# All stores of two steps ahead of the keys, and positions between gelus: one edit to a convolution and window-attention kernel

## The chip, the cores and the metric

The kernel runs on one core of a Trainium2 chip. The time is device microseconds of one execution; lower is better. The core has a tensor engine (TensorE, PE in the profile), VectorE (DVE), ScalarE (ACT), GpSimd (POOL) and SyncE (SP), which here only issues DMA transfers. Each engine works through its own list of instructions in order, and semaphores tie the lists together.

## What is computed

The input x has shape (4, 16, 512, 512), float32. Four layers follow each other; the edit is in the first one, layer 0:

```python
pos = depthwise_conv3x3(x, pos_w)                 # one filter a channel
x = x + pos + pos_b
y = (x @ color1.T) * alpha1 + beta1               # tokens of 16 channels
q, k, v = split(windows_8x8(y) @ qkv_w.T + qkv_b) # 2 heads of 8 channels
out = softmax(q * 8**-0.5 @ k.T) @ v              # inside each 8 x 8 window
x = x + out @ proj_w.T + proj_b
h = gelu(((x @ color2.T) * alpha2 + beta2) @ fc1_w.T + fc1_b)   # 64 hidden
x = x + h @ fc2_w.T + fc2_b
```

Layer 1 quantizes x and its weights to 8 bits, convolves 3 x 3, normalizes over the batch and clips to 0 to 6. Layer 2 is two 3 x 3 convolutions with a relu between them and a residual sum. Layer 3 is a 3 x 3 convolution, a perceptron with 128 hidden channels and a residual sum. The kernel returns the float32 result of layer 3.

## The kernel before

Layer 0 is the function `window_attention`. It runs 64 steps, n = 0 to 63. A step covers, for each of the 4 images (index u) and each of 8 strips of the picture, 8 rows by 64 columns, which is 8 windows. The strips lie on the partitions: four groups of 32 (index vv), each with two strips of 16 channels.

All lists of instructions are in the order of the source (a manual schedule, no planner). A step is put together from these parts, by their names in the code:

- `depthwise(n, tap, u)` (L287): four small matmuls that add one of nine taps for image u into PSUM bank u. Banks 0 and 1 are one tile (`pairs[0]`), banks 2 and 3 another (`pairs[1]`).
- `position(n)`: when all 36 groups of a step are issued, VectorE copies banks 0 and 1 (L302) and ScalarE banks 2 and 3 (L298) with the bias into a tile `y`.
- `turn_keys(y, vv)` (L310): eight DMA transfers of 32 KB that bring one fourth of `y` into the tile `y2`, by which keys and values are read. They are the "keys". They go through SP.
- `query` (L319): the queries, multiplied with the key weights, into the tile `g`.
- `values(k)` (L338): four transposes of `y2` into bank 4 or 6, copied on into a tile `yt`. `scores(k, n)` (L353): the scores of one eighth of the step into banks 0 to 3, and their exponentials on ScalarE (L361). `attend` (L374) multiplies exponentials and values; `divide` (L389 to L396) and `turn_back` (L403) bring the result into the tile `o`.
- `project(y)` (L409, L414): the output projection and the residual sum into `y`.
- `hidden(y, u, vv, b, n)` (L421): a perceptron block, four matmuls into one of banks 4 to 7 and a gelu on ScalarE (L426). A step has 16.
- `output(...)` (L432, L437): the second half of the perceptron for 16 blocks, and four sums by VectorE into the tile `xo`. It is issued in the next step, behind `scores(0)`.

The work of several steps is interleaved: step n attends its own windows, turns the keys of step n + 1, and forms the depthwise sums of step n + 2. `xo` holds two steps side by side: the even one writes the left half of its columns, the odd one the right half; there is a single buffer (L554). `output` of an odd step is issued in the even step behind it, and there `store` puts 32 stores of 64 KB on a list. `send(k)` takes up to k stores from the list and issues them on SP (L90). `highest_output` (L452) takes the absolute maximum of one eighth of `xo` on VectorE.

The middle of a step is a loop over k = 1 to 7. At its end, in this order: the keys of step n + 1 (at k = 1, 3, 5 and 7), one `highest_output`, and `send(5)` (L537 to L539). An even step so issues 8 keys and 10 stores in turn, and 2 stores at the end; an odd step has no stores. Behind all this SP issues the load of x for step n + 4 (1320 KB, L185).

The end of a step is written as a string (L561). Its letter at place i stands for a depthwise group (d), a perceptron block (h) or a query (q), and i % 4 gives the group of 32 rows of the array that it uses, the image of a d and the vv of an h. Perceptron blocks take banks 6, 7, 4 and 5 in turn. With the last d `position(n + 2)` is issued at once. The last thing of a step on ScalarE is the table load for the exponentials (L574); the load for gelus is at L540.

Of the kernel before, what the change touches and what calls it, by code (L numbers as in the profile page):

```python
# [86 lines left out]
def _store_block(nc, x1, src, b, r0, cols, queues=None):  # L87

    rows = x1.rearrange("m (r c) b x -> (m r) c b x", r=2)[r0 + 1 : r0 + 1 + WS, :, b, cols]
    (next(queues) if queues else nc.sync).dma_start(rows.rearrange("m c x -> c m x"), src)  # L90
# [53 lines left out]
def window_attention(ctx: ExitStack, tc, xw, x1, hots, m, v, peak):  # L144
# [15 lines left out]
    U = V = 4  # L160
# [122 lines left out]
    def depthwise(n, tap, u):  # L283

        dy, dx = divmod(tap, 3)
        for vv in range(V):
            nc.tensor.matmul(  # L287
                bank(u)[quad(vv)], taps[quad(u), tap, :],
                xts[n][quad(u), vv, dy : dy + WS, dx : dx + BW],
                start=tap == 0, stop=tap == 8,  # L290
            )

    def position(n):

        y = px.tile([P, U, N], F32, tag="y", name=f"y{n}", bufs=3)
        for u in range(U):
            if u // 2:
                nc.scalar.activation(  # L298
                    by_window(y[:, u]), by_row(bank(u)), AF.Identity, bias=v("pos_b")
                )  # L300
            else:
                nc.vector.tensor_scalar(  # L302
                    by_window(y[:, u]), by_row(bank(u)), v("pos_b"), None, ALU.add
                )
        return y

    def turn_keys(y, vv):
        for u in range(U):
            for w in range(2):
                nc.sync.dma_start(  # L310
                    y2[32 * u + C * w : 32 * u + C * w + C, vv, :, w, :],
                    y[32 * vv + C * w : 32 * vv + C * w + C, u, :].rearrange(
                        "p (j t) -> p j t", t=T
                    ),
                )

    def query(y, h, vv, b, scalar=False):
        for u in range(U):
            nc.tensor.matmul(  # L319
                b[quad(u)], wg[h][quad(vv)], y[quad(vv), u, :], start=True, stop=True  # L320
            )
        out, src = g[:, vv, :, h, :], b.rearrange("p (j t) -> p j t", t=T)
        if scalar:
            nc.scalar.activation(out, src, AF.Identity, bias=gb[:, h : h + 1])
        else:
            nc.vector.tensor_scalar(out, src, gb[:, h : h + 1], None, ALU.add)
# [6 lines left out]
    def values(k):  # L333

        vv, jl = k // 2, 4 * (k % 2)
        b, t = bank(4 + 2 * (k % 2)), yts[k % 3]
        for jj in range(4):
            nc.tensor.transpose(  # L338
                b[:, P * jj : P * jj + P],
                y2[:, vv, jl + jj].rearrange("p w t -> p (w t)"), m("ident"),  # L340
            )
        src = b.rearrange("p (a w c) -> p a w c", w=2, c=C)
        if 0 < k < 7:
            nc.scalar.copy(t[:, :, 0:3:2], src)
        else:
            nc.vector.tensor_copy(t[:, :, 0:3:2], src)  # L346

    def scores(k, n):

        vv, jl = k // 2, 4 * (k % 2)  # L350
        for i, jj in ((0, 0), (0, 1), (1, 0), (0, 2), (1, 1), (0, 3), (1, 2), (1, 3)):
            for u in (2 * i, 2 * i + 1):
                nc.tensor.matmul(  # L353
                    bank(u)[:, P * jj : P * jj + P],
                    y2[quad(u), vv, jl + jj].rearrange("p w t -> p (w t)"),
                    g[quad(u), vv, jl + jj].rearrange("p h t -> p (h t)"),
                    start=True, stop=True,
                )
        e = px.tile([P, U, 4, P], F32, tag="e", name=f"e{n}_{k}", bufs=3)
        for i in range(2):  # L360
            nc.scalar.activation(  # L361
                e[:, 2 * i : 2 * i + 2].rearrange("p u j t -> p u (j t)"),
                pairs[i], AF.Exp,
            )
        return e

    def attend(e, k):

        t = yts[k % 3]
        for jj in range(4):  # L370
            for u in range(U):
                for w in range(2):
                    half = slice(64 * w, 64 * w + 64)
                    nc.tensor.matmul(  # L374
                        bank(4 + 2 * (k % 2) + w)[quad(u), P * jj : P * jj + P],
                        t[half, U * jj + u, w : w + 2].rearrange("p d c -> p (d c)"),
                        e[half, u, jj, :],
                        start=True, stop=True,
                    )

    def part(t, k):
        vv, jl = k // 2, 4 * (k % 2)
        return t[:, vv, jl : jl + 4].rearrange("p j h t -> p (j h t)")
# [18 lines left out]
    def turn_back(t, k):  # L402
        nc.vector.transpose(part(o, k), t.rearrange("p b w c -> p (b w c)"))  # L403
# [25 lines left out]
    def output(y, xo, hids, us, banks, n):  # L429

        for k, (vv, hd) in enumerate(hids):
            nc.tensor.matmul(  # L432
                bank(banks[k // 4])[quad(vv)], m("fc2"), hd, start=True, stop=True
            )
        at = BW * (n % 2)
        for u, i in zip(us, banks):
            nc.vector.tensor_tensor(  # L437
                xo[:, u, :, at : at + BW].rearrange("p a (j x) -> p a j x", x=WS),
                by_window(bank(i)), by_window(y[:, u]), ALU.add,
            )  # L440
        if n % 2:
            store(xo, n // 2, us)
# [22 lines left out]
    def send(k, queues=None):  # L465
        for _ in range(min(k, len(stores))):
            src, u, r, cb = stores.pop(0)
            _store_block(nc, x1, src, u, r, slice(XW * cb, XW * cb + XW), queues)
# [40 lines left out]
    for n in range(STEPS):  # L509
        more, ahead = n + 1 < STEPS, n + 2 < STEPS  # L510
        taken, asked = [0] * U, [0] * V

        def block(what, i, b, scalar=False):
            at = i % 4
            if what == "q" and more:
                query(ys[n + 1], asked[at], at, b, scalar)
                asked[at] += 1
            elif what == "d" and ahead:
                depthwise(n + 2, taken[at], at)
                taken[at] += 1  # L520
                if taken == [9] * U:
                    ys[n + 2] = position(n + 2)

        values(0)
        es, ts = {0: scores(0, n)}, {}
        if last:

            output(*last)
        for k in range(1, 8):
            es[k] = scores(k, n)  # L530
            values(k)
            attend(es[k - 1], k - 1)
            ts[k - 1] = divide(k - 1, n, nc.gpsimd)
            if 1 < k < 7:
                turn_back(ts[k - 2], k - 2)
            if k % 2 and more:
                turn_keys(ys[n + 1], k // 2)  # L537
            highest_output()
            send(5)  # L539
        nc.scalar.preload_act_table_set("gelu_and_others")  # L540
        attend(es[7], 7)
        ts[7] = divide(7, n, nc.gpsimd)
        for k in (5, 6, 7):
            turn_back(ts[k], k)
        free = iter((4, 5, 6, 7, 4, 5))
        for i, what in enumerate("qqddddqqqqdddddd"):
            block(what, i, bank(next(free)) if what == "q" else None, True)
        if more:
            highest(n + 1)
        highest_output()  # L550
        y = ys.pop(n)
        project(y)
        if n % 2 == 0:
            xo = px.tile([P, U, WS, XW], F32, tag="xo", name=f"xo{n}", bufs=1)  # L554
        if not more:
            flag = bounded()

        hids, units = [], itertools.cycle((6, 7, 4, 5))  # L560
        for i, what in enumerate("ddddhdhddhqhddhqhddhdhddhdhddhdhddhdhddddhdh"):  # L561
            if what == "h":
                q = len(hids)
                hids.append(hidden(y, q // 4, i % 4, bank(next(units)), n))
                if not more and q in (5, 9, 13):
                    u = q // 4 - 1
                    output(y, xo, hids[q - 5 : q - 1], (u,), (u,), n)
                    send(8, queues)
            else:
                block(what, i, bank(next(units)) if what == "q" else None)  # L570
        if n + 4 < STEPS:
            xts[n + 4] = load(n + 4)
        if more:
            nc.scalar.preload_act_table_set("natural_log_exp_and_others")  # L574
        last = (y, xo, hids, range(U), (5, 4, 6, 7), n)
# [797 lines left out]
```

## Time and profile before

| | us |
|---|---|
| median of 3 runs | 5752.89 |
| lowest and highest of them | 5740.05, 5767.73 |
| the profiled execution | 5755.15 |
| its span, first to last instruction | 5753.4 |
| TensorE busy | 5477.8 |
| VectorE busy | 3734.7 |
| ScalarE busy | 3491.1 |
| layer 0, to the end of the last sum of L437 | 3262.6 |
| granted TensorE clock, mean | 0.987 |

How to read it: the busy times are of the whole span, and the engines work side by side. A row of the waits or of the timeline gives an engine, a source line, what is written and read (out<-in, without buffer numbers) and, in square brackets, the idle time of the engine just before and what ended it. Where several semaphores are waited for, the profile names the one that it sees come last, which can be the wrong one. PEld is the load of weights into the array, SPq and DVEq are the engines' sequencers, which issue transfers and wait. The times of the timeline count from the start of the span. A table load of L574 every 48 to 53 us marks the steps: the one at 1015.78 us ends step 18, the one at 1066.67 step 19, the one at 1116.14 step 20. The mean length of the odd steps 3 to 61 is 50.14 us, of the even steps 2 to 62 49.43 us.

### The profile page before, as it was taken

To read this page: it belongs to the slowest core of one execution; us is meant where nothing else is said; L and a number is where in the kernel's file an instruction comes from. 1 tells how busy PE (TensorE), PEld (TensorE's weight loads), DVE (VectorE), ACT (ScalarE), POOL (GpSimd) and SP (SyncE) were. 2 spreads that over 40 slices of the span, in tenths; PEclk is the share of its full clock that TensorE was granted. 3 is DMA by queue.
4 is the path that set the end of the run, shared out by engine and by line. 5 is a ranking of instruction groups with operands and counts; after the bars stand their busy time and mean duration, and the time that the engine had idled before them with its cause. 6 is when DMAs were issued, how large, how long until landed. Compare 5 with 4: busy or idle time off the path is not lost. (4 is left out here: it accounts for less than half of the span.)

```text
span 5753.4 us, 268539 instructions
## 1 busy us (share of the span) xinstructions
PE 5477.8 (95%) x120912; PEld 2921.8 (51%) x120912; DVE 3734.7 (65%) x5806; ACT 3491.1 (61%) x4739; POOL 707.3 (12%) x692
## 2 busy tenths in 40 slices
PE   7999999999999999999999776999999999999999
PEld 5666666666666666666666433322222322223222
DVE  4666666666666666666666565676676766767666
ACT  3777767777777777677777554444444444444444
POOL 1111111111111111111111253000000000000000
PEclk9999999999999999999999898999999999999999
DMA  2332323333332323333332497776777777677774
GB/s 79 70 79 67 76 65 78 74 74 76 71 79 68 81 62 76 73 73 76 71 78 48 96 257 202 177 173 175 176 174 177 174 174 176 173 177 174 174 175 110
DMA packets 626194, 677.47 MB, mean 118 GB/s; under 512 B 355856, under 2 KB 485008, under 8 KB 616848
## 3 DMA queue, kind: packets, MB, share of 16 engines
q1 hardware_dynamic: 624240, 658.76, 47.6%
q8 instruction: 953, 15.61, 1.2%
q14 instruction: 201, 1.65, 0.1%
q0 software_dynamic: 512, 1.05, 0.1%
q10 hardware_dynamic: 288, 0.39, 0.0%
HBM read 222.45 MB, written 134.48 MB: 62 GB/s over the span
## 5 line engine op out<-in xcount | busy, mean ns | idle before, releaser
L361 ACT ACTIVATE e<-pair 128x1024 f32<-128x1024 f32 x1024 | 992.8, 1022 | 449.2 <-PE pair L353 448.5
L287 PE MATMUL pair<-x,taps 32*32 32x512 f32 x18432 | 1081.7, 600 | 3.7 <-issue 2.3
L1205 ACT ACTIVATE hid<-tb,vec 128x512 f32<-128x512 f32 x1024 | 646.8, 684 | 630.7 <-PE tb L1197 630.7
L389 DVE STREAM_TRANSPOSE a<-bank 128x512 f32<-128x512 f32 x1024 | 669.8, 692 | 354.2 <-PE bank L374 327.6
L396 POOL TENSOR_TENSOR t<-a,r 128x512 f32<-128x512 f32 x512 | 542.0, 1059 | 2679.3 <-DVE r L394 2615.6
L426 ACT ACTIVATE hid<-bank,f1b 128x512 f32<-128x512 f32 x1024 | 648.1, 687 | 346.0 <-PE bank L421 282.2
L353 PE MATMUL pair<-g,y 32*128 32x128 f32 x16384 | 764.0, 288 | 31.1 <-ACT y L298 25.3
L353 PEld LDWEIGHTS pair<-g,y 32*128 32x128 f32 x16384 | 650.8, 188 | 192.5 <-issue 76.1
L421 PE MATMUL bank<-y,fc_e 32*32 32x512 f32 x8192 | 738.4, 606 | 1.0 <-DVE y L414 1.0
L1207 DVE TENSOR_SCALAR hid<-tb,vec 128x512 f32<-128x512 f32 x1024 | 718.0, 744 | 27.2 <-PE tb L1197 26.9
L374 PE MATMUL bank<-e,yt 64*32 64x128 f32 x32768 | 611.8, 276 | 29.7 <-DVE yt L346 21.1
L1197 PE MATMUL tb<-ye,mat 32*128 32x512 f32 x4096 | 586.2, 640 | 0.0
L287 PEld LDWEIGHTS pair<-x,taps 32*32 32x32 f32 x18432 | 493.4, 103 | 175.5 <-issue 71.2
L374 PEld LDWEIGHTS bank<-e,yt 64*32 64x32 f32 x32768 | 466.9, 106 | 129.0 <-issue 101.9
L1217 PE MATMUL tb<-hid,mat 128*32 128x512 f32 x4096 | 466.0, 595 | 0.0
L1122 PE MATMUL tb<-zo,cw 64*32 64x512 f32 x3096 | 368.2, 601 | 16.7 <-issue 8.9
L338 PE MATMUL bank<-mat,y 128*128 128x128 f32 x2048 | 340.3, 289 | 44.1 <-DVE xo L437 44.1
L1122 PE MATMUL tb<-xo,cw 64*32 64x512 f32 x3096 | 360.3, 592 | 3.7 <-issue 2.2
L1122 PE MATMUL tb<-ho,cw 64*32 64x512 f32 x3072 | 358.0, 593 | 4.6 <-issue 3.0
L1122 PE MATMUL tb<-ze,cw 64*32 64x512 f32 x3072 | 362.2, 601 | 0.0
L1122 PE MATMUL tb<-he,cw 64*32 64x512 f32 x3072 | 357.9, 593 | 0.0
L1122 PE MATMUL tb<-xe,cw 64*32 64x512 f32 x3072 | 355.9, 593 | 0.0
(180 smaller groups left out, 6809.9 us busy)
## 6 DMA issues: line engine op xcount, KB each, us to landing
x<-in_xw_dram SPq DMA_DIRECT2D x64, 1320.0 KB
zo<-ze SPq DMA_DIRECT2D x512, 128.5 KB
ho<-he SPq DMA_DIRECT2D x512, 128.5 KB
xo<-xe SPq DMA_DIRECT2D x512, 128.5 KB
y<-y SPq DMA_DIRECT2D x2048, 32.0 KB
tx<-x SPq DMA_DIRECT2D x256, 256.0 KB
out_dram<-xe SPq DMA_DIRECT2D x128, 512.0 KB
x<-xo SPq DMA_DIRECT2D x1008, 64.0 KB
```

Of the source, the lines that this page charges most:

```text
L287: nc.tensor.matmul(bank(u)[quad(vv)], taps[quad(u), tap, :], xts[n][quad(u), vv, dy : dy + WS, dx : dx + BW], start=tap == 0, stop=tap == 8,)
L353: nc.tensor.matmul(bank(u)[:, P * jj : P * jj + P], y2[quad(u), vv, jl + jj].rearrange("p w t -> p (w t)"), g[quad(u), vv, jl + jj].rearra ...
L361: nc.scalar.activation(e[:, 2 * i : 2 * i + 2].rearrange("p u j t -> p u (j t)"), pairs[i], AF.Exp,)
L374: nc.tensor.matmul(bank(4 + 2 * (k % 2) + w)[quad(u), P * jj : P * jj + P], t[half, U * jj + u, w : w + 2].rearrange("p d c -> p (d c)"), ...
L389: nc.vector.transpose(a[:, 512 * w : 512 * w + 512], bank(4 + 2 * (k % 2) + w))
L396: engine.tensor_tensor(t.rearrange("p b w c -> p w b c"), top, r.unsqueeze(3).to_broadcast([P, 2, 16, C]), ALU.mult,)
L421: nc.tensor.matmul(b[quad(k)], fc1[quad(vv), quad(k)], y[quad(vv), u, :], start=True, stop=True,)
L426: nc.scalar.activation(hd, b, AF.Gelu, bias=f1b)
L1122: nc.tensor.matmul(p[r][_quad(2 * f + w)], weights[_half(r), odd, dx, :], src[_half(r), f, dx : dx + W], start=dx == 0, stop=dx == 2,)
L1197: nc.tensor.matmul(p[q], w1[_quad(q), 1 - par, :], inner(src)[_quad(q), f, :], start=True, stop=True,)
L1205: nc.scalar.activation(hd, p[q], AF.Relu, bias=v("l3_b1"))
L1207: nc.vector.tensor_scalar(hd, p[q], v("l3_b1"), 0.0, ALU.add, ALU.max)
```

## The change

There are two edits, both in `window_attention`.

The stores are no longer sent five at a time in each round of k. All 32 on the list are sent in the round k = 1, in front of the first keys. In an odd step the list is empty and nothing is sent.

In the string that ends a step, one h moves from place 34 to 33, and the tail changes. The h's of the tail stood at places 34, 36, 41 and 43, with the last d at 42; they now stand at 33, 36, 42 and 43, with the last d at 41. The last two perceptron blocks so follow the last depthwise group, and on ScalarE the two positions stand in front of the last two gelus instead of between them. The last d of banks 2 and 3 moves from place 42 to 39, that of banks 0 and 1 from 40 to 41. The numbers of d, h and q are the same.

```diff
@@ -533,10 +533,11 @@
             ts[k - 1] = divide(k - 1, n, nc.gpsimd)
             if 1 < k < 7:
                 turn_back(ts[k - 2], k - 2)
+            if k == 1:
+                send(8 * U)
             if k % 2 and more:
                 turn_keys(ys[n + 1], k // 2)
             highest_output()
-            send(5)
         nc.scalar.preload_act_table_set("gelu_and_others")
         attend(es[7], 7)
         ts[7] = divide(7, n, nc.gpsimd)
@@ -558,7 +559,7 @@
 
 
         hids, units = [], itertools.cycle((6, 7, 4, 5))
-        for i, what in enumerate("ddddhdhddhqhddhqhddhdhddhdhddhdhddhdhddddhdh"):
+        for i, what in enumerate("ddddhdhddhqhddhqhddhdhddhdhddhdhdhddhdddddhh"):
             if what == "h":
                 q = len(hids)
                 hids.append(hidden(y, q // 4, i % 4, bank(next(units)), n))
```

## The prediction

> **What bounds the kernel now.** The page came first. TensorE is busy for 5477.8 of 5753.4 us, so whatever is gained must come out of its idle or slow time. The page's chain names only lines of layers 1 to 3 (L1122, L1197, L1217), and the change is in layer 0, so I went on to the waits between 200 and 3100 us, the steady part of layer 0. Columns: engine and line, what it waited for, us in total, times, longest.
>
> ```profile
> DVE xo L437 <- DMA x<-xo: 111.0, 19, 7.9
> ...
> PE bank L338 <- DVE xo L437: 42.4, 27, 3.5
> ...
> PE pair L353 <- ACT y L298: 23.6, 58, 0.4
> ```
>
> VectorE waits for the stores of `xo` to land before it may overwrite `xo`; TensorE then waits for VectorE; and in another place TensorE waits 0.4 us in every step for ScalarE's positions. These are the two places that the diff touches. The timeline of the SP queue shows why the stores are late:
>
> ```profile
> 1003.77 6.56 SPq L90 DMA_DIRECT2D x<-xo  x10
> 1010.43 7.36 SPq L310 DMA_DIRECT2D y<-y  x8
> 1017.83 1.07 SPq L90 DMA_DIRECT2D x<-xo  x2
> ```
>
> SP issues stores (L90) and keys (L310) one after another without a pause from 972.6 us; the last two stores go out at 1017.8, while the step itself ended at 1015.8 (the table load of L574, the last thing a step does on ScalarE). In the next step, an odd one, VectorE and TensorE pay for it:
>
> ```profile
> 1014.19 0.69 DVE L346 COPY yt<-bank 128x512 f32<-128x512 f32 x1
> 1021.60 2.48 DVE L437 TENSOR_TENSOR xo<-bank,y 128x512 f32<-128x512 f32 x4 [6.71 <-PE pair L353]
> ```
>
> ```profile
> 1019.90 1.27 PE L353 MATMUL pair<-g,y 32*128 32x128 f32 x32
> 1023.54 0.66 PE L338 MATMUL bank<-mat,y 128*128 128x128 f32 x4 [2.37 <-DVE xo L437]
> ```
>
> The four sums start 5.8 us after the table load; in the even step behind it they start 1.7 us after it (1068.41 against 1066.67). The named releaser, scores of L353, had ended by then; the last store's packets end at 1020.3, so this wait belongs to the stores too. TensorE stands at `values(1)` (L338) because its bank 6 is still unread by L437. Over all steps that is 44.1 us of TensorE idle time in 28 cases, all odd steps.
>
> The length of a step, from one table load of L574 to the next, for an odd step with the stall, the even one behind it, and one of the two odd steps (31 and 51) in which the stores happened to land in time (columns: window, length, busy time of each engine, clock, DMA):
>
> ```profile
> 1015.80:1066.70 50.90, 47.55 (x1386) 32.80 (x1380) 29.46 (x47) 35.82 (x49) 8.46 (x8) 1.00 0.26 63
> 1066.70:1116.10 49.40, 48.74 (x1384) 33.56 (x1378) 34.24 (x55) 35.82 (x48) 8.48 (x8) 1.00 0.39 84
> ```
>
> ```profile
> 1609.20:1656.90 47.70, 47.03 (x1384) 34.31 (x1380) 29.65 (x47) 35.79 (x48) 8.47 (x8) 1.00 0.26 64
> ```
>
> **Part 1, the stores in one go.** Nothing is added or removed: an even step still issues 32 stores and 32 keys. In the new order SP issues all stores before the first key. They need only the sums of L437, which in an even step end 1.7 to 5.0 us after the table load; keys had to wait until 6.0. At the mean spacing of a store (6.56 us for ten) the 32 take 21.0 us and the last is out near +24, landed by +26. The next write of `xo` comes near +49.5: 23 us of room instead of none. So the wait of L437 goes.
>
> Its worth: the 30 odd steps from 3 to 61 average 50.14 us. The five with the least stall, less that stall (47.71, 47.91, 48.14, 48.78, 48.33), average 48.17. 30 x 1.97 is 59 us, and 2 more for step 63: **61 us**. 44 of it are the idle time itself. About 15 are the clock, which in steady layer 0 is halved only in these odd steps:
>
> ```profile
> 821.40:824.80 3.40, 3.40 (x82) 2.68 (x84) 1.05 (x3) 0.58 (x1) 0.00 (x0) 0.50 0.40 140
> 2313.00:2316.40 3.40, 3.04 (x72) 2.33 (x72) 0.91 (x2) 0.65 (x2) 0.00 (x0) 0.50 0.49 193
> ```
>
> There are seven such stretches (steps 15, 39, 41, 45, 47, 53, 59), 30.8 us in all at 0.50, hence 15.4 us lost. Each starts between 1.1 us before and 1.5 us behind the end of a stall of 1.7 to 3.5 us. The Trainium skill ("TensorE: Matmul & The Clock Gate", Part 1) says that the clock is halved after an idle window of about 3.4 us. Taken so, only the stall of 3.5 us in step 41 explains its drop; the other six would have another cause and stay, leaving 61 - 13.7 = 47 us. The trace has no drop in any even step, so I take the row, 61, and keep 47 as an end.
>
> What is pushed back: the keys. SP is free for the first key near +24 instead of +6. 32 keys at 0.77 us (24.71 us for 32 in an odd step) end near +48, about where they end now (+49.5). The first eight are issued by +30 and their packets end about 2 us later. `values(0)` of the next step reads them near +46, `scores(2)` the next eight some 9 us later, and so on: at least 14 us of cover for each group, so the cost is nothing. Without that cover TensorE waits at a step's first instruction and everything waits. The x load behind them leaves near +48, not +51, and is read a whole step later. A page speaks against the new order: "DMA: Bandwidth & Descriptors" (Queues, rings and completion order) has an engine take descriptors in ring order, so no key can overtake 2.1 MB of stores. By the rate in the same page (Anatomy of one DMA, 436 GB/s; an estimate) the stores move in 4.8 us; by the row, SP needs 21 us to issue them. The row is the longer one and is what I used, so the rule adds nothing to it.
>
> **Part 2, the end of the string.** The number of depthwise groups (d) and hidden blocks (h) is the same, and each place keeps its row group (i % 4); only what stands there changes. The old tail is h d h (places 41 to 43), the new one d h h; one h also comes forward from place 34 to 33, into a run in which ScalarE has gelus queued, and costs nothing (its bank 4 was freed by a gelu ending near 1060.6, the place comes near 1061.1). The old tail:
>
> ```profile
> 1064.24 0.69 ACT L426 ACTIVATE hid<-bank,f1b 128x512 f32<-128x512 f32 x1 [0.76 <-PE bank L421]
> 1064.83 1.25 ACT L298 ACTIVATE y<-pair,vec 128x512 f32<-128x512 f32 x2
> 1065.96 0.70 ACT L426 ACTIVATE hid<-bank,f1b 128x512 f32<-128x512 f32 x1
> 1066.67 1.28 ACT L574 ACT_TABLE_LOAD   x1
> ```
>
> ```profile
> 1064.99 0.71 PE L353 MATMUL pair<-g,y 32*128 32x128 f32 x8
> 1066.13 1.16 PE L353 MATMUL pair<-g,y 32*128 32x128 f32 x24 [0.42 <-ACT y L298]
> 1067.22 3.64 PE L432 MATMUL bank<-hid,mat 128*32 128x512 f32 x32
> ```
>
> `scores(0)` needs banks 2 and 3 read by ScalarE (until 1066.08); that is the 0.42. In the new order the last d of banks 2 and 3 is at place 39, and no gelu stands ahead of the positions: ScalarE starts them at 1063.48, when the gelu run ends, and is done at 1064.75. The two gelus then end at 1066.05, 0.6 us earlier than now; that gains nothing, since TensorE, not ScalarE, holds the next exponentials (2.15 us of idle before them). But the last d, at 41, now belongs to bank 1. VectorE's two positions share one wait for banks 0 and 1. They start at 1063.53 now, behind place 40, and then behind place 41, whose block ends at 1064.20: end 1065.62 instead of 1064.94. `scores(0)` starts 0.68 later, at 1065.67, but runs through: its second part starts after 8 rows at 0.032 us, at 1065.93 against 1066.13. Gain 0.2 us, times 62 steps: **12 us**. Bounds: VectorE's wait vanishes too, the whole 0.42: 26 us gained; place 41 ends 0.4 us later than I read: 12 us lost. I take 12, worked out from the trace's own places.
>
> **Sum.** 5753.4 - 61 - 12 = 5680 us. The profiled execution took 5755.15 us, its span is 5753.4, the median of the three runs 5752.89; the span stands for the median, so 5680 is the forecast.
>
> **Rivals.** (B) The wait goes, but the clock drops and other small delays of the odd steps stay, and part 2 gives nothing or a little less: only the 44 us of idle time come back, 5753 - 44 = 5709, up to 5721. For it: steps 27 and 35 were 49.0 with stalls of 0.7 and 0.2. Against it: every drop sits at a stall. (C) More comes back: all odd steps run at 47.8 (72 us) and part 2 gives 26: 5655. For it: steps 31 and 51. (D) Slower, by late keys. Stores issued in a long run may space out; of the single stores some take 1.5 us to issue, most 0.48. `values(0)` would wait once 32 stores take over 35 us (46 less 2.5, 6.2 for eight keys and 2 to land), 1.1 us each, and the gain of 73 us is used up at 1.17 us each (a wait of 2.4 us in 31 steps). At 1.25 us it is 4.7 us a step, 146 us: 5826. Against it: ten in a row kept 0.66. (E) The change does not do what it says, because L437 waited for TensorE as its row says: only the 12 us, 5741. Against it: in each odd step L437 starts 0.7 to 1.5 us behind the last store's packets.
>
> **How the numbers follow.** My forecast 0.70 (own range 5662 to 5698), B 0.14, C 0.07, D 0.05, E 0.04. A measurement of this kernel can tell about 0.5%, 29 us, from no change. Below 5724 lie the forecast, C and nearly all of B: 0.90. E and the rest of B are within: 0.05. D is slower: 0.05. The range takes in C and most of B and leaves D and E out: 5648 to 5716.
>
> **What would show it.** Right: the SP queue of even steps has 32 stores, then 32 keys; no wait of L437 for stores and none of L338 for L437; odd steps near 48, shorter than the even ones at 49.2; no clock drops in odd steps; L298 in front of two gelus and no 0.42 before L353, but a wait of L353 for L302 of some 0.6. Wrong: waits of L338 or L353 at a step's start for keys, stores spaced over 1 us, or odd steps that stay at 50.

## The result and the profile after

The changed kernel takes 5686.99 us (median of four runs, 5666.78 to 5699.29) where the kernel before, in four runs, takes 5760.31 us (5740.05 to 5770.55). The ratio is 0.987, 95% interval 0.983 to 0.992: faster by 1.3%. The forecast was 5680 us. The profiled execution has a span of 5691.6 us against 5753.4 us, 61.8 us less.

First the waits of the changed kernel between 200 and 3100 us (engine and line, what it waited for, us in total, times, longest):

```profile
DVE xo L437 <- issue: 105.6, 57, 1.9
...
PE pair L353 <- DVE y L302: 43.7, 60, 0.7
...
DVE xo L437 <- PE bank L432: 25.5, 117, 1.9
```

Two rows of before are gone altogether: L437 waits for no store, and L338 not for L437. The longest wait that L437 has left is 2.2 us. The 0.4 us of L353 for ScalarE have become 0.7 us for VectorE. The SP queue of an even step and of the odd one behind it:

```profile
1045.23 20.86 SPq L90 DMA_DIRECT2D x<-xo  x32
1066.21 26.53 SPq L310 DMA_DIRECT2D y<-y  x32
1092.84 0.54 SPq L185 DMA_DIRECT2D x<-in_xw_dram  x1
1098.43 26.29 SPq L310 DMA_DIRECT2D y<-y  x32
```

The step begins at 1042.2. Its last store is out 23.9 us later, and `xo` is written again 51.9 us after the begin. The odd step 19 and the even step 20 (window, length, busy time of each engine, clock, DMA):

```profile
994.30:1042.20 47.90, 46.95 (x1380) 33.71 (x1380) 29.76 (x48) 35.62 (x48) 8.47 (x8) 1.00 0.21 55
1042.20:1091.90 49.70, 47.95 (x1380) 33.36 (x1383) 34.36 (x56) 35.80 (x50) 8.47 (x8) 1.00 0.42 90
```

Step 19 took 50.9 us before. The odd steps 3 to 61 now average 48.0 us instead of 50.1, the even ones 49.2 instead of 49.4. The end of step 20, TensorE and then ScalarE (start, length, what; in brackets the idle time in front; L575 is L574 of the kernel before):

```profile
1090.38 0.66 PE L338 MATMUL bank<-mat,y 128*128 128x128 f32 x4
1091.76 1.27 PE L353 MATMUL pair<-g,y 32*128 32x128 f32 x32 [0.72 <-DVE y L302]
1092.96 3.64 PE L432 MATMUL bank<-hid,mat 128*32 128x512 f32 x32
```

```profile
1089.43 1.28 ACT L298 ACTIVATE y<-pair,vec 128x512 f32<-128x512 f32 x2
1090.58 1.28 ACT L426 ACTIVATE hid<-bank,f1b 128x512 f32<-128x512 f32 x2
1091.88 1.28 ACT L575 ACT_TABLE_LOAD   x1
```

The positions stand in front of both gelus, and `scores(0)` starts later but runs through, as forecast.

Where the 61.8 us come from: layer 0 ends at 3190.1 us instead of 3262.6, 72.5 us earlier. The next stretch, the first pass over layer 0's result, took 307.3 us instead of 296.9, 10.4 us more. The rest took 2194.1 against 2193.9.

### The profile page after: what moved, and what is told of

Read it like the earlier page. It is cut to its first block, busy times and chain, and to the rows that moved or that the text cites. A ratio compares the mean times of both kernels' runs of the same rounds, so it can differ in the third digit from the quotient of the medians.

```text
span 5691.6 us, 268539 instructions
## 1 busy us (share of the span) xinstructions
PE 5428.8 (95%) x120912; PEld 2891.5 (51%) x120912; DVE 3738.1 (66%) x5806; ACT 3482.3 (61%) x4739; POOL 707.5 (12%) x692
## 3 DMA queue, kind: packets, MB, share of 16 engines
q1 hardware_dynamic: 624240, 658.76, 48.2%
## 5 line engine op out<-in xcount | busy, mean ns | idle before, releaser
L353 PE MATMUL pair<-g,y 32*128 32x128 f32 x16384 | 727.4, 287 | 50.2 <-DVE y L302 45.2
L353 PEld LDWEIGHTS pair<-g,y 32*128 32x128 f32 x16384 | 626.2, 186 | 198.1 <-issue 131.8
L421 PE MATMUL bank<-y,fc_e 32*32 32x512 f32 x8192 | 709.2, 606 | 1.0 <-DVE y L414 1.0
L374 PE MATMUL bank<-e,yt 64*32 64x128 f32 x32768 | 608.2, 274 | 28.1 <-DVE yt L346 21.0
L374 PEld LDWEIGHTS bank<-e,yt 64*32 64x32 f32 x32768 | 463.3, 106 | 128.3 <-issue 105.0
L302 DVE TENSOR_SCALAR y<-pair,vec 128x512 f32<-128x512 f32 x128 | 90.2, 746 | 413.2 <-PE pair L287 413.2
```

The source lines that it names most:

```text
L353: nc.tensor.matmul(bank(u)[:, P * jj : P * jj + P], y2[quad(u), vv, jl + jj].rearrange("p w t -> p (w t)"), g[quad(u), vv, jl + jj].rearra ...
L374: nc.tensor.matmul(bank(4 + 2 * (k % 2) + w)[quad(u), P * jj : P * jj + P], t[half, U * jj + u, w : w + 2].rearrange("p d c -> p (d c)"), ...
L421: nc.tensor.matmul(b[quad(k)], fc1[quad(vv), quad(k)], y[quad(vv), u, :], start=True, stop=True,)
```

## The experiments

One table for all kernels that ran. "Layer 0" is the end of the last sum of L437 in the trace; "drops" are the stretches at half clock from step 2 up to step 61; "first pass" runs from the end of layer 0 to the end of layer 1's statistics. Ratios are to the kernel before on the same chip. A kernel without a ratio was run once and is read from its trace alone.

| kernel | ratio, 95% interval | layer 0, us | odd, even step | drops | first pass |
|---|---|---|---|---|---|
| before | 1 | 3262.6 | 50.1, 49.4 | 7 | 296.9 |
| before_again | | 3269.9 | 50.4, 49.4 | 7 | 293.3 |
| changed | 0.987 (0.983, 0.992) | 3190.1 | 48.0, 49.2 | 0 | 307.3 |
| after_again | 0.986 (0.983, 0.989) | 3196.3 | 48.2, 49.3 | 1 | 308.4 |
| stores_only | 0.994 (0.991, 0.996) | 3202.2 | 48.2, 49.4 | 0 | 304.7 |
| string_only | 0.998 (0.997, 0.999) | 3232.5 | 49.9, 48.9 | 9 | 302.8 |
| send6 | 0.992 (0.989, 0.995) | 3187.7 | 48.3, 49.0 | 0 | 298.3 |
| tail_hhh | 0.981 (0.977, 0.985) | 3150.4 | 47.5, 48.4 | 0 | 305.3 |
| peak_early | 0.986 (0.983, 0.989) | 3183.5 | 48.1, 48.9 | 0 | 301.2 |
| best | 0.976 (0.973, 0.979) | 3150.1 | 47.7, 48.2 | 0 | 309.0 |
| keys_reversed | | 3836.9 | 48.1, 69.9 | 30 | 292.5 |
| stores_half_more | | 3252.1 | 50.2, 49.2 | 9 | 305.2 |
| stores_twice | | 3409.8 | 55.3, 49.1 | 38 | 304.6 |
| half_more_load_pool | | 3186.7 | 47.9, 49.2 | 0 | 302.2 |

**The stores alone.** The string is that of before:

```diff
-        for i, what in enumerate("ddddhdhddhqhddhqhddhdhddhdhddhdhdhddhdddddhh"):
+        for i, what in enumerate("ddddhdhddhqhddhqhddhdhddhdhddhdhddhdhddddhdh"):
```

> Part 1 alone; the string of the kernel before. Forecast theory (the wait of L437 was for the last stores, and the clock drops were its consequence): no wait of L437 for stores, odd steps near 48.2, no clock drop before step 62, layer 0 shorter by 52 to 61 us, time near 5697. Rival (L437 waited for the scores of TensorE, as its row says): odd steps stay at 50, time near 5755. Rival (the clock drops have a cause of their own): odd steps near 48.7, five or more drops of 3.4 us stay, layer 0 shorter by 45 us.

Layer 0 ended 60.4 us earlier than before, the odd steps average 48.2 us, no clock drop is left, and no wait of L437 for a store. The rival in which L437 waited for TensorE is out, and so is the one in which the drops stand by themselves. In time the ratio is worth 20 to 53 us, less than the 60 of layer 0; the first pass is again some 8 us longer than in the first trace of before (see the end).

**The string alone.** The stores go five at a time, as in the kernel before; against that kernel the edit is:

```diff
-        for i, what in enumerate("ddddhdhddhqhddhqhddhdhddhdhddhdhddhdhddddhdh"):
+        for i, what in enumerate("ddddhdhddhqhddhqhddhdhddhdhddhdhdhddhdddddhh"):
```

> Part 2 alone; stores five at a time as before. Forecast theory: the idle time of 0.42 us in front of the second part of scores(0) becomes one of 0.7 us in front of the first, and a step gains 0.2 to 0.3 us: 12 to 20 us over 62 steps, time near 5742. Waits of L437 for stores stay in the odd steps, and with them clock drops, some five to eight. Rival (the change gives nothing, since VectorE's later positions take back what ScalarE gains): within 5 us of before.

The ratio of 0.998 (0.997 to 0.999) is 4 to 18 us, 11 in the middle. The waits between 200 and 3100 us hold both the old stall and the new wait:

```profile
PE bank L338 <- DVE xo L437: 44.9, 26, 4.2
PE pair L353 <- DVE y L302: 43.0, 59, 0.7
DVE xo L437 <- DMA x<-xo: 37.7, 8, 6.1
```

(The rest of L437's late starts is put down to other engines, as before.) Nine clock drops, two of them here (window, length, busy times, clock, DMA):

```profile
1015.10:1021.90 6.80, 5.99 (x104) 4.89 (x104) 3.02 (x6) 1.64 (x3) 1.05 (x1) 0.50 0.30 97
1117.50:1120.90 3.40, 3.40 (x89) 2.75 (x90) 1.21 (x3) 0.59 (x1) 0.00 (x0) 0.50 0.23 60
```

With the late stores the drops are back.

**Six at a time behind the keys.** Is it the one go that counts, or only that the last store leaves ahead of the last keys?

```diff
-            if k == 1:
-                send(8 * U)
             if k % 2 and more:
                 turn_keys(ys[n + 1], k // 2)
             highest_output()
+            send(6)
```

> The changed kernel, but with six stores in each round of k behind the keys, instead of all 32 ahead of them: the last two leave at k = 6, ahead of the last eight keys. Theory (all that counts is that the last store leaves before the next write of xo by a few us): the last store leaves near +43 to +45 of the even step and has landed before +49.5, no wait of L437, odd steps near 48, time as the changed kernel, 5687 within 15. Rival (it takes the one go: SP loses time in alternating, or the margin is needed): waits of L437 in half or more of the odd steps, odd steps near 49, time near 5710.

The SP queue of step 20:

```profile
1055.80 7.55 SPq L90 DMA_DIRECT2D x<-xo  x12
...
1070.11 7.68 SPq L90 DMA_DIRECT2D x<-xo  x12
...
1083.56 4.90 SPq L90 DMA_DIRECT2D x<-xo  x8
1088.56 7.47 SPq L310 DMA_DIRECT2D y<-y  x8
```

The last store is out at 1088.5, in the median of the even steps at +45.6 (+51.7 in the kernel before). No wait of L437 for stores, no drop, layer 0 at 3187.7, as in the changed kernel. In the original order SP issues keys and stores without a pause from the first key on, in step 18 from 972.6 to 1018.9, and two stores stand behind the last eight keys, whose issue takes 7.4 us. Taking these two past the keys is worth the whole of part 1 in layer 0. Sending all in front is not needed. In time the ratio is worth 29 to 61 us. The changed kernel, 0.987 and 0.986 on other chips, did not run on this one, so that the two are equally fast is shown for layer 0 alone.

**Another tail.** If the 0.7 us in front of `scores(0)` come from the last depthwise group at place 41, one that ends at 40 should free them:

```diff
-        for i, what in enumerate("ddddhdhddhqhddhqhddhdhddhdhddhdhdhddhdddddhh"):
+        for i, what in enumerate("ddddhdhddhqhddhqhddhdhddhdhddhdhddddhddddhhh"):
```

> The changed kernel with another tail: places 32 to 43 are d d d d h d d d d h h h, so that the last depthwise groups are at 39 (banks 2, 3) and 40 (banks 0, 1), and three perceptron blocks follow them. Theory (the 0.7 us before scores(0) is the wait for VectorE's positions behind place 41): positions of VectorE start 0.7 us earlier, TensorE does not wait at L353, 62 times 0.7 is 43 us, time near 5645. Rival (ScalarE sets the end of a step: its three gelus behind the positions put off the table load and the exponentials): steps as long as in the changed kernel or longer, time 5687 or more.

Ratio 0.981, layer 0 another 40 to 46 us earlier. TensorE and ScalarE at the end of step 19:

```profile
1078.95 0.66 PE L338 MATMUL bank<-mat,y 128*128 128x128 f32 x4
1079.64 1.27 PE L353 MATMUL pair<-g,y 32*128 32x128 f32 x32
1080.85 3.64 PE L432 MATMUL bank<-hid,mat 128*32 128x512 f32 x32
```

```profile
1078.00 1.27 ACT L298 ACTIVATE y<-pair,vec 128x512 f32<-128x512 f32 x2
1079.15 1.85 ACT L426 ACTIVATE hid<-bank,f1b 128x512 f32<-128x512 f32 x3
1081.02 1.28 ACT L575 ACT_TABLE_LOAD   x1
```

No idle time is left between transposes, scores and `output`. ScalarE's table load comes later in relation to the scores and costs nothing. So the wait was VectorE's, and 62 x 0.7 = 43 us was its price.

**The eighth maximum of an even step, earlier.** With and without the tail:

```diff
-            highest_output()
+            highest_output(2 if k == 1 else 1)
...
             highest(n + 1)
-        highest_output()
```

> The changed kernel with only the eighth absolute maximum of xo moved from the tail to k = 1. Theory: the tail of an even step falls from 22.6 us to 22.0 or less, even steps near 48.2, layer 0 shorter by 20 to 37 us than in the changed kernel. Rival: VectorE is short of time at k = 1 and the gain is given back there, layer 0 as in the changed kernel.

> The changed kernel with the tail of tail_hhh, and the eighth absolute maximum of xo taken at k = 1 (two there) instead of in the tail of the step. Theory (in the tail of an even step VectorE's reduction of 0.64 us stands ahead of the four sums of L414 for which TensorE waits): tails of even steps shorter by 0.6 to 1.2 us, 20 to 37 us on top of tail_hhh, ratio to the kernel before near 0.976. Rival (TensorE has other work in that place): as tail_hhh, ratio 0.981.

A miss. Beside the changed kernel on the same chip peak_early's ratio is 0.986 against 0.986, its layer 0 7 to 13 us shorter, the tail of its even steps 22.4 us against 22.7. With the better tail it gives nothing: 3150.1 against 3150.4. Why even steps are a microsecond longer than odd ones stays open. As the fastest version, 0.976 of before, "best" owes its gain to the tail.

**Late keys.** First a badly built try:

```diff
-                turn_keys(ys[n + 1], k // 2)
+                turn_keys(ys[n + 1], 3 - k // 2)
```

> The changed kernel with a step's four groups of keys turned in the opposite order, so that SP waits at its first key for the last reading of y2 (k = 7, near +25) and the group that the next step reads first is issued last, near +44 to +50. Theory (late keys stop TensorE at the start of a step, the rival D of the forecast): values(0) waits for keys, 5 to 6 us in each step, and the clock is halved behind most of these stops (1.7 us each): 62 times 7 us, near 6100 us. Rival (there is cover that I did not see): the time of the changed kernel, within 30 us.

In this kernel the groups 3 and 2 are turned at k = 1 and 3, ahead of their last reading in the same step. So it takes the keys and values of half of a step's windows from the next step, and waits in the same step for them, not at the start of the next, as I had written. Even steps, whose keys stand behind the 32 stores, took 69.9 us and TensorE waited in them for keys:

```profile
PE pair L353 <- DMA y<-y: 413.1, 84, 16.4
```

The odd ones stayed at 48.1. It shows what late keys cost, 20 us a step with the clock, but not where the edge is. That needs more stores in front of keys in their right order. Once 32 stores (stores_twice) and once 16 (stores_half_more) were issued a second time, the same data to the same place. The edit for 16; for 32 it reads `again = list(stores)` and `send(8 * U)`:

```diff
             if k == 1:
+                again = stores[4 * U :]
                 send(8 * U)
+                stores.extend(again)
+                send(4 * U)
```

> The changed kernel with all 32 stores issued twice ahead of the keys. Theory: the first key leaves near +44, the first eight have landed near +52, values(0) of the odd step wants them near +45: TensorE waits about 7 us in each of 31 odd steps, and the clock is halved behind most of these waits: layer 0 longer by 220 to 280 us than in the changed kernel. Rival (there is no such edge): longer by less than 50 us.

> The changed kernel with the last 16 of the 32 stores issued a second time, ahead of the keys. Theory (the forecast's account of the cover): 48 stores at 0.65 us put the first key near +34, the first eight have landed near +42, values(0) reads them near +45: no wait for keys, layer 0 as in the changed kernel, 3190 to 3196 us, within 10. Rival (the cover is smaller than that): waits for keys at the start of odd steps, layer 0 longer by 50 us or more.

With 64 stores the last is out at +43.3 in the median, and the edge is there: layer 0 213 to 220 us longer, where 220 to 280 were expected. The waits between 200 and 3100 us, with `values(0)` waiting for keys:

```profile
PE bank L338 <- DMA y<-y: 102.3, 27, 5.5
...
PE bank L374 <- issue: 30.9, 35, 3.1
```

The second row is a loss of another kind, which the next kernel shows more plainly; late keys are only a part of the 213 us.

With 48 stores, the last out at +33.1, TensorE waits for no key, as expected. But layer 0 was 56 to 62 us longer all the same, which I had not expected. Odd steps were back at 50.2 us, with nine clock drops. The place, in step 17, which begins at 914.4:

```profile
926.91 1.11 PE L374 MATMUL bank<-e,yt 64*32 64x128 f32 x58
931.53 0.41 PE L374 MATMUL bank<-e,yt 64*32 64x128 f32 x6 [3.51 <-issue]
```

The clock behind it:

```profile
932.10:935.50 3.40, 3.40 (x60) 2.84 (x65) 2.19 (x4) 1.59 (x2) 1.06 (x1) 0.50 0.20 39
```

TensorE stands for 3.51 us in the middle of 64 equal matmuls, with no semaphore to wait for ("issue"). There are 31 such gaps of over 0.6 us, 44.0 us in all; in the changed kernel six, 4.3 us; in stores_twice 31 again, 46.6 us. In the DMA packets of the trace, each of the 31 ends 1.2 to 1.7 us behind the end of a 16 KB packet on the instruction queue. That queue moved 953 such packets for 243 578 records of TensorE, 256 to a packet, and counted in the order of the records all 31 gaps stand at the same place of a run of 256, within one. So what TensorE waits for there is its next packet of instructions. In step 17 these packets start at +6.2 and +14.7; in the changed kernel at +6.0, +10.9 and +15.2. And between them lies the x load, whose packets run from +9.7 to +14.7:

```profile
899.10 23.65 SPq L310 DMA_DIRECT2D y<-y  x31
922.85 0.54 SPq L185 DMA_DIRECT2D x<-in_xw_dram  x1
923.49 27.39 SPq L310 DMA_DIRECT2D y<-y  x32
```

The later keys have pushed it from about the end of the even step to 8.5 us into the odd one. To tell the load from the stores and keys, GpSimd issues it instead of SP, and all else stays:

```diff
-            xts[n + 4] = load(n + 4)
+            xts[n + 4] = load(n + 4, nc.gpsimd)
```

> stores_half_more with the load of x for step n + 4 issued by GpSimd instead of SP, so that it leaves when the depthwise groups of a step are done, near the end of the step, and not behind SP's backlog 8 us into the odd step. Theory (the x load holds up the fetch of TensorE's instructions, and TensorE stood without instructions for 1 to 3.5 us near +17 of the odd steps): these gaps go, odd steps back near 48.2, layer 0 near 3195, within 10. Rival (the longer run of stores and the later keys themselves make the gaps): layer 0 stays near 3250.

The waits of TensorE with issue at L374, first with the load on SP, then on GpSimd:

```profile
PE bank L374 <- issue: 36.9, 42, 3.5
```

```profile
PE bank L374 <- issue: 6.8, 15, 0.7
```

Layer 0 ended at 3186.7, odd steps took 47.9 us, six gaps of 4.3 us in all, no clock drop. The same 48 stores and late keys cost nothing once the x load leaves in time, 47.7 us after the begin of an even step in the median instead of 57.8. So the load in that place made the gaps; that it delays the fetch of TensorE's instructions is what the packets show. The load changed its queue as well as its place, but in the changed kernel it leaves from SP, at 48.7, without these gaps, so the place is what counts.

**Both kernels once more.**

> The changed kernel once more, for a second trace and for a comparison on the same chip. Layer 0 ends within 5 us of 3190 us; no clock drop before step 62; the first pass over layer 0's result differs by up to 10 us from the 307 us of its first trace, if that pass varies from run to run by itself, and is the same if the change has lengthened it.

> The kernel before once more, for a second trace. Layer 0 ends within 15 us of 3263 us, with waits of L437 for stores in most odd steps and five to nine drops of the clock in odd steps alone. The first pass over layer 0's result, 297 us in the first trace: the same within 2 us if the change is what lengthens it (307 us there), up to 10 us more if it varies by itself.

Layer 0 repeats within 6 and 7 us. The first pass took 307 and 308 us in the two traces of the changed kernel and 297 and 293 in those of before, so it doesn't look like mere scatter, and on this point the theory of a free variation fell. It is not settled: the four kernels with stores between the keys have 293 to 303 us, the others 301 to 309, but keys_reversed, with its stores in one go, has 292.5. The instructions of that pass are the same everywhere. What moves it I didn't find.

## Why the prediction was right, point by point

- **That L437 waits for the last stores, though its row names TensorE: right.** stores_only takes the wait away by moving stores alone, send6 by sending six at a time (with the new string), and odd steps fall to 48.2 and 48.3; 48.17 had been read from the least stalled steps. Two places were read some 2 us early: in step 20 the next write of `xo` comes at +51.9, not near +49.5, and the last keys are out at +50.5, not near +48. Against 23 us of room for the stores and 14 for the keys that changed nothing.
- **Part 1, 61 us: right in layer 0.** 60.4 us between the first trace of before and stores_only, 67.7 from the second trace.
- **The clock, row against rule: the row was right.** With the stalls there are 7, 7 and 9 drops. Without them there is none in seven kernels and one in after_again, which starts 0.1 us behind the end of a stall of 1.6 us that ends with issue. In stores_half_more nine stalls of this other kind, eight of them under 3.4 us, brought nine drops. The rule that the forecast quotes, read as the least stall that costs clock, left out 13.7 us of the gain; but no drop stayed behind.
- **The keys' cover, at least 14 us: about right for the keys.** 16 stores more, about 10 us, cause no wait for keys; 32 more, about 20 us, cause one of 2 to 6 us in odd steps. Rival D placed its edge at stores that take 35 us; it lies between 30 us (48 stores) and 41 us (64). The change is far from it, since its 32 stores took 20.9 us in step 20 (21.0 in the forecast). The page that the forecast cites here, "DMA: Bandwidth & Descriptors" of the Trainium skill, gives ring order for the start of transfers and lets a later one finish first (Queues, rings and completion order), and it gives the 436 GB/s for DMAs from GpSimd (Anatomy of one DMA), while these stores go through SP. Nothing hung on either, since SP's 20.9 us are the longer time.
- **"The x load is read a whole step later": the one weak step.** The conclusion held, because the load moved forward (in the median of the even steps to 48.7 us after their begin, from 51.8), but the reason given was not enough. A load that nobody reads soon still has a place in which it does harm, at 57.8 in stores_half_more and 67.1 in stores_twice, and the forecast had no term for that.
- **Part 2, 12 us: right in its mechanism, small in its size.** VectorE's positions start behind place 41, and TensorE waits 0.72 us for them (0.68 in the forecast). From the end of the last perceptron block to the end of `scores(0)` it is 2.58 us instead of 2.91: 0.33 us gained, not 0.2, since the 32 matmuls run through in 1.27 us, where I had added 0.26 and 1.16. That would be 20 us. string_only shows 4 to 18 us in time, 30 to 37 in layer 0, and on top of the stores layer 0 shows 6 to 12, so its size is no better known than that.
- **The sum.** 73 us forecast, 72.5 measured in layer 0. The second traces make it anything from 66 to 80, so that it came within half a microsecond is luck; both parts are known to some 7 us. In time the medians differ by 73.3 us (48 to 97 by the interval). The time lies 7 us above 5680 because the forecast counted from the 5753.4 us of one execution, and four runs of the kernel before have a median of 5760.31. The 10 us that the first pass took back in the profiled execution had no term in the forecast.

## What to carry to other kernels

In an in-order queue of transfers the last few decide, not the sum: two stores behind eight keys, at the end of a queue that never paused, held up a whole step, and in layer 0 moving these two was worth as much as moving all. Work out what a short stall brings with it, such as half a clock for 3.4 us or more, from the kernel's own drops. Ask of each transfer that is pushed back not only who reads it, but what else it will meet there; a large load can stop an engine that doesn't read it at all. Where an idle time ends with "issue", look at the packets of the instruction queue.

## What was not expected of the hardware

- A load of 1320 KB in packets of 10.3 KB delayed the 16 KB fetches on the instruction queue by about 4 us (one started at +14.7, with the load's last packet just ended, instead of +10.9), and TensorE ran out of instructions for up to 3.5 us. The row in the profile is idle time that ends with "issue".
- The half clock follows stalls that stand amid dense work and last 1.6 us or more (1.6 to 4.2 us in the kernels before, before_again, string_only, stores_half_more and after_again), in stretches of 3.4 or 6.8 us that start within 2.4 us of the stall's end. Not every such stall has one: in step 13 of the kernel before, one of 2.7 us had none.
- The rate of the first pass, which reads the stores' result at 240 to 280 GB/s, differs by up to 6% between kernels that do the same there; the cause is open.
